# Two fused transformer layers on one core: dummy products before the first rows, a quantized up group moved behind the third down tile, and one copy moved to VectorE

## The chip, the cores and the metric

The kernel runs on one NeuronCore of a Trainium2 chip. The core has a matrix engine (TensorE, PE in the profile), three elementwise engines (VectorE = DVE, ScalarE = ACT, GpSimd = POOL) and SyncE (SP), which issues the DMA transfers. The metric is the device time of one execution in microseconds (us), taken as the median of several runs. Every engine runs its own instructions in the order of the program and waits for the others through semaphores.

## The reference, cut to what matters

Four blocks follow each other on x of 2 batches x 512 rows x 512 columns, all in float32. Each block ends with a residual addition and a layer norm.

```python
x = norm(x + attn0(x))   # linear attention: q = elu(x Wq + bq) + 1, then (q M) / (q z), then Wo
x = norm(x + ffn0(x))    # ternary weights: trunc(clip(128 * silu(gate) * up)), down, trunc(clip)
x = norm(x + attn1(x))   # one head of 128: softmax(q k^T / sqrt(128)) v, then Wo and a bias
x = norm(x + ffn1(x))    # silu(x Wg) * (x Wu), then Wd, in full float32 weights
```

## The kernel before, in words

A batch is four tiles of 128 rows. TensorE contracts over partitions, so every block first transposes its rows (products with an identity matrix into PSUM, then a copy to SBUF) and then runs the products with the weights. PSUM has eight buffers, shared by all products in turn (`psum`, line 68). The order of the work on PE, ACT, DVE and SP comes from a scheduler, which sorts the instructions by its own idea of when each could run; GpSimd's order is that of the source (`manual_schedule`, line 59). Once sorted, each engine keeps its order whatever happens.

**The start (lines 80 to 123 and 270 to 325).** SP issues the loads of the four row tiles of batch 0, of `bq` and `z` (128 x 8 each), and of the eight query weights `wq`. PE transposes the row tiles as they land (line 110, 16 transposes into four PSUM buffers), ACT and DVE copy two of the four buffers each (lines 121 and 123), and the query products follow (line 316). `bq` is first read by ACT (line 321), `z` by a copy on POOL (line 310).

**The end of the quantized feed-forward (lines 506 to 662).** `up(b, c)` is one group of 128 (the last: 96) of the 1376 inner columns for batch b: 16 products for gate and up, then on ACT a silu (529), on DVE a product (532) and a cut (149), on ACT two truncating conversions (159, 160) and on DVE their sum (539). `f0_down(i)` issues the down product of row tile i (0 to 3 are batch 0, 4 to 7 batch 1; 11 products, line 569) and keeps a pipeline going behind it:

- `scaled(i)`: ACT scales the sum out of PSUM (586) and DVE cuts it (149);
- `added(i - 1)`: ACT converts twice (159, 160), DVE combines them to `w` (594), POOL subtracts `w` from the rows (595);
- `layernorm_stats` of tile i - 2 on DVE (129, 131), with the root on POOL (137, 138);
- `layernorm_apply` of tile i - 3 on DVE (143).

The rows of batch 0 are then transposed for the next attention (`xt_a1`, line 110), copied (121, 123) and multiplied by the query and key weights (line 746).

**The second attention (lines 735 to 885).** For each batch the probabilities are transposed (`pt_p`), `values` multiplies them with v into one PSUM buffer (line 814) and copies the result to `ot` (line 818, on ACT for both batches), and four `output` products (line 831) follow. `attended` adds the residual and takes the norm's statistics on DVE (836, 129, 131); the root and offset are made on POOL (137, 138, 825, 826), and ACT applies the norm (827). `split_rows(0)` then transposes the normed rows of batch 0 (line 860) and cuts them into parts on DVE and ACT (669, 688 to 690) for the last feed-forward's products (line 906).

Of the kernel before, what the change touches and what calls it, by code (L numbers as in the profile page):

```python
# [19 lines left out]
P = 128  # L20
# [16 lines left out]
def kernel(  # L37
# [19 lines left out]
    nc = tc.nc  # L57
# [10 lines left out]
    def psum(name):  # L68
        return ps.tile([P, 512], F32, tag="mm", name=name)
# [4 lines left out]
    def load_x(b):  # L74
        for t in range(NT):
            x = xp.tile([P, HID], F32, tag="x", name=f"x_{b}_{t}")
            nc.sync.dma_start(x, x_in[b, ts(t, P), :])
            xs[b].append(x)

    load_x(0)  # L80
    bq = const.tile([D, NH], F32, tag="bq", name="bq")
    nc.sync.dma_start(bq, bq_in)
    z = const.tile([D, NH], F32, tag="z", name="z")
    nc.sync.dma_start(z, z_in)

    ident = const.tile([P, P], F32, tag="ident", name="ident")
    make_identity(nc, ident)
# [7 lines left out]
    nc.vector.memset(below_half, -BELOW_HALF)  # L95
    ones = const.tile([P, P], F32, tag="ones", name="ones")
    nc.vector.memset(ones, 1.0)


    copies = []  # L100
# [25 lines left out]
    def layernorm_stats(row, name):  # L126

        st = small.tile([P, 6], F32, tag="st", name=f"st_{name}")
        nc.vector.bn_stats(st, row)
        mv = small.tile([P, 2], F32, tag="mv", name=f"mv_{name}", bufs=8)  # L130
        nc.vector.bn_aggr(mv, st)
        return root(mv, name)
# [8 lines left out]
    def layernorm_apply(out, row, stats):  # L141
        mv, rstd = stats
        nc.vector.tensor_scalar(
            out, row, mv[:, 0:1], rstd, ALU.subtract, ALU.mult
        )
# [76 lines left out]
    def branch(flag):  # L222
        return nc.values_load(flag[0:1, 0:1], engines=[PE], min_val=0, max_val=1)
# [44 lines left out]
    def query_tile(name):  # L268
        return wqp.tile([P, 2, HID], F32, tag="wq", name=name)

    with tc.tile_pool(name="a0w", bufs=1) as a0w, tc.tile_pool(name="a0", bufs=2) as a0:
        wq = []
        for h in range(NH):
            if h % 2 == 0:
                two = query_tile(f"wq{h}").rearrange("p a (k d) -> p a k d", k=NK)
            w = two[:, h % 2]
            nc.sync.dma_start(w, wq_in[h])
            wq.append(w)
        load_x(1)
        m = a0w.tile([D, NH, D], F32, tag="m", name="m")  # L280
        nc.sync.dma_start(m, m_in)
# [169 lines left out]
        order = [(b, t) for b in range(B) for t in range(NT)]  # L451
# [49 lines left out]
    with tc.tile_pool(name="f0", bufs=2) as f0:  # L501
# [7 lines left out]
        def up(b, c):  # L509
            n = CHUNKS[c][1]  # L510
            t = ts_up[c]
            pp = [psum(f"pg_f0{b}_{c}"), psum(f"pu_f0{b}_{c}")]
            with tc.If(ternary_up > 0) as way:
                for a in range(2):
                    for i in range(2 * NK):
                        nc.tensor.matmul(  # L516
                            pp[a][:n], t[:, a, i % NK, :n], x2[b][i],
                            start=(i == 0), stop=(i == 2 * NK - 1),
                        )
            with way.Else():  # L520
                for a in range(2):
                    for i in range(2 * NK):
                        nc.tensor.matmul(
                            pp[a][:n], gus[c][:, a, i % NK, :],
                            x2[b][i].bitcast(F32),
                            start=(i == 0), stop=(i == 2 * NK - 1),
                        )
            sg = fp.tile([P, S], F32, tag="sg", name=f"sg_f0{b}_{c}")
            nc.scalar.activation(sg[:n], pp[0][:n], AF.Silu, scale=silu_scale[:n])
            y = f0.tile([P, S], F32, tag="y", name=f"y_f0{b}_{c}")  # L530

            step = nc.vector.scalar_tensor_tensor(
                y[:n], sg[:n], eff_up[:n, 1:2], pp[1][:n], ALU.mult, ALU.mult
            )
            cut_to_12(y[:n])
            ta, tb = truncated_parts(f0, y[:n], n, f"f0{b}_{c}")

            it = its[b][c // 4][:, c % 4]
            nc.vector.scalar_tensor_tensor(  # L539
                it[:n], tb[:n], 128.0, ta[:n], ALU.min, ALU.subtract  # L540
            )
            inter[b].append(it)
            if to_divide:
                part = to_divide.pop(0)
                if part:
                    divided(*part)
            return step
# [16 lines left out]
        def down(b, t):  # L564
            pd = psum(f"pd_f0{b}_{t}")
            last = len(CHUNKS) - 1
            with tc.If(ternary_d > 0) as way:
                for c, (_, n) in enumerate(CHUNKS):
                    nc.tensor.matmul(  # L569
                        pd, inter[b][c][:n, ts(t, P)], td[c][:n].bitcast(F32R),  # L570
                        start=(c == 0), stop=(c == last),
                    )
            with way.Else():
                for c, (_, n) in enumerate(CHUNKS):
                    nc.tensor.matmul(
                        pd, inter[b][c][:n, ts(t, P)].bitcast(F32), wds[c][:n],
                        start=(c == 0), stop=(c == last),
                    )
            return pd
# [4 lines left out]
        def scaled(i):  # L584
            y = f0.tile([P, HID], F32, tag="y", name=f"yd_{i}")
            nc.scalar.activation(y, pds[i], AF.Copy, scale=down_scale)
            cut_to_12(y)
            ys[i] = y

        def added(i):  # L590
            b, t = order[i]
            ta, tb = truncated_parts(f0, ys[i], P, f"d{i}")
            w = fp.tile([P, HID], F32, tag="sg", name=f"w_{i}")
            nc.vector.scalar_tensor_tensor(w, tb, 128.0, ta, ALU.min, ALU.subtract)  # L594
            nc.gpsimd.tensor_sub(xs[b][t], xs[b][t], w)  # L595

        def f0_down(i):
            if i < len(order):
                pds[i] = down(*order[i])
                scaled(i)  # L600
            if 0 <= i - 1 < len(order):
                added(i - 1)
            if 0 <= i - 2 < len(order):
                b, t = order[i - 2]
                stats[i - 2] = layernorm_stats(xs[b][t], f"f0_{i - 2}")
            if 0 <= i - 3 < len(order):
                b, t = order[i - 3]
                layernorm_apply(xs[b][t], xs[b][t], stats[i - 3])
# [30 lines left out]
        nc.vector.tensor_scalar(down_scale, eff_d, -128.0, None, ALU.mult)  # L639
        up(1, 9)  # L640
        ternary_d = branch(flag_d)
        f0_down(0)
        f0_down(1)
        up(1, 10)
        for i in range(2, len(order) - 1):
            f0_down(i)
        xt_a1 = [transposed(xs[0], "a10")]
        for i in range(len(order) - 1, len(order) + 3):
# [83 lines left out]
    for b in range(B):  # L732
# [10 lines left out]
        for j in range(2):  # L743
            p = psum(f"pqk_{b}_{j}")
            for k in range(NK):
                nc.tensor.matmul(  # L746
                    p, wqkv[:, k, ts(j, D)], xt[:, k, :],
                    start=(k == 0), stop=(k == NK - 1),
# [7 lines left out]
        for t in range(NT):  # L756
            p = psum(f"pv_{b}_{t}")
            for k in range(NK):
                nc.tensor.matmul(  # L759
                    p[:, :D], xt[:, k, ts(t, P)], wqkv[:, k, ts(2, D)],  # L760
                    start=(k == 0), stop=(k == NK - 1),
# [49 lines left out]
    def values(b, pt):  # L811
        po = psum(f"pot_{b}")
        for k in range(NT):
            nc.tensor.matmul(
                po, qkv[b][2][:, k, :], pt[:, k, :], start=(k == 0), stop=(k == NT - 1)
            )
        ot = ot2[:, b, :]
        nc.scalar.copy(ot, po)
        ots.append(ot)

    def scalar_norm(x, stats, name):
# [32 lines left out]
    def split_rows(b, room):  # L854
# [9 lines left out]
        return parts  # L864

    values(0, pt0)
    pt1 = transposed(probs[1][0], "p1")
    for t in range(NT):
        attended(0, t, output(0, t))
    values(1, pt1)  # L870
    sums1 = [output(1, t) for t in range(NT)]
    rooms = [rows_room(0, "r0"), None]
# [221 lines left out]
```

## Time and profile before

| | us |
|---|---|
| median of 3 runs | 492.82 (492.47 to 493.49) |
| the profiled execution, whole | 495.07 |
| its span, from first to last instruction | 493.3 |
| PE busy | 475.6 (96%) |
| DVE busy | 350.4 (71%) |
| ACT busy | 272.1 (55%) |
| POOL busy | 127.3 (26%) |
| granted clock of TensorE, mean | 0.991 |

The profiled execution is 2.25 us longer than the median of the runs. All start times are counted from the start of its span. A row of a timeline gives start, duration, engine, line, operation, what is written and read, and how often; in brackets stands how long the engine had been idle and what ended that. A float32 product with 512 columns appears as two matmul instructions of about 0.43 us each from start to start.

### The profile page before, as it was taken

The page shows a single profiled execution, that of the slowest core. Times are in us where ns is not written, and L with a number is a line of the kernel's source. Part 1 is how long each engine was busy: PE and PEld are TensorE (multiplying, and loading weights), DVE is VectorE, ACT ScalarE, POOL GpSimd, SP SyncE. Part 2 cuts the span into 40 slices and gives each one's busy share as a digit, 9 for nine tenths or more (in the row PEclk, how much of TensorE's full clock was granted, in tenths as well). Part 3 has the DMA queues.
Part 4 walks back from the last instruction along what each step waited for, and adds up shares of the span by engine and source line. Part 5 has one row for each costly group of instructions (what it writes and reads, how often), then busy time and mean ns, then how long its engine had stood idle before and what let it go on. Part 6 is the DMA issues. An engine that isn't in the chain of part 4 may idle for free.

```text
span 493.3 us, 5751 instructions
## 1 busy us (share of the span) xinstructions
PE 475.6 (96%) x1859; PEld 325.1 (66%) x1859; DVE 350.4 (71%) x672; ACT 272.1 (55%) x507; POOL 127.3 (26%) x163
## 2 busy tenths in 40 slices
PE   6999999999999999999899978999999999999995
PEld 4454444434577788777566536788778888888885
DVE  1374677677675576846869968888876697999852
ACT  1444899565677576456545933556655565433220
POOL 0253102666520194003874033000000000023211
PEclk9999999999999999999999989999999999999998
DMA  8999600000060001121670000000000000000111
GB/s 280 400 361 355 238 1 0 1 0 1 2 200 31 3 1 45 46 87 33 203 282 2 0 0 1 1 0 2 0 1 0 1 1 1 1 21 23 43 45 43
DMA packets 13749, 33.99 MB, mean 69 GB/s; under 512 B 1872, under 2 KB 2768, under 8 KB 13712
## 3 DMA queue, kind: packets, MB, share of 16 engines
q1 hardware_dynamic: 13568, 33.37, 18.9%
q8 instruction: 22, 0.36, 0.3%
q10 hardware_dynamic: 144, 0.13, 0.1%
q14 instruction: 15, 0.12, 0.1%
HBM read 31.40 MB, written 2.10 MB: 68 GB/s over the span
## 4 chain that ended last, share of the span: by engine, by line
PE 65%; DVE 9%; ACT 8%; issue 3%; POOL 2%; POOLq 0%; DVEq 0%; ACTq 0%
PE pm L906 16%; PE pdm L981 8%; PE pu_f L516 8%; PE pg_f L516 8%; PE pc L906 8%; PE pdc L981 4%; DVE x L382 4%; PE pqk L746 3%; ACT y L373 2%; ACT t L392 2%; PE pd_f L569 2%; PE pv L759 1%; PE psc L773 1%; PE po L360 1%; ACT den L364 1%
## 5 line engine op out<-in xcount | busy, mean ns | idle before, releaser
L360 PE MATMUL po<-mw,q 128*128 128x512 f32 x128 | 56.7, 597 | 1.1 <-DVE x L382 0.9
L316 PE MATMUL pq<-xt_a,wq 128*128 128x512 f32 x128 | 57.3, 600 | 0.0
L360 PEld LDWEIGHTS po<-mw,q 128*128 128x128 f32 x128 | 23.2, 189 | 33.2 <-issue 18.9
L316 PEld LDWEIGHTS pq<-xt_a,wq 128*128 128x128 f32 x128 | 24.4, 193 | 30.0 <-issue 27.8
L137 POOL TENSOR_TENSOR rstd_f<-mv_f,ln_eps 128x1 f32<-128x1 f32 x16 | 4.0, 252 | 139.9 <-DVE mv_f L992 137.6
L906 PE MATMUL pm<-r,it_early 128*128 128x512 f32 x144 | 38.2, 394 | 0.2
L906 PE MATMUL pm<-r,ugu 128*128 128x512 f32 (+1 forms) x144 | 36.8, 393 | 0.0
L382 DVE SCALAR_TENSOR_TENSOR x<-po,den,x 128x511 f32<-128x511 f32 x40 | 29.8, 746 | 2.0
L906 PEld LDWEIGHTS pm<-r,it_early 128*128 128x128 f32 x144 | 26.9, 188 | 6.6 <-ACT r L688 0.4
L906 PEld LDWEIGHTS pm<-r,ugu 128*128 128x128 f32 (+1 forms) x144 | 26.8, 186 | 6.3
L159 ACT ACTIVATE ta_f<-y_f,below_half 128x512 int8<-128x512 f32 (+1 forms) x22 | 15.9, 722 | 25.8 <-DVE y_f L149 25.5
L917 DVE SCALAR_TENSOR_TENSOR ev_q<-pm,ev_q 128x512 f32<-128x512 f32 (+1 forms) x28 | 19.2, 687 | 14.0 <-PE pm L906 14.0
L377 POOL TENSOR_TENSOR y<-y,y 128x511 f32<-128x511 f32 x16 | 20.3, 1271 | 32.1 <-ACT y L373 31.3
L394 POOL TENSOR_SCALAR td<-wd,inv_down 128x512 fp32r<-128x512 f32 (+1 forms) x11 | 19.5, 1791 | 30.3 <-DVE inv_down L193 30.3
L539 DVE SCALAR_TENSOR_TENSOR it_f<-tb_f,ta_f 128x512 fp32r<-128x512 int16 (+1 forms) x22 | 15.1, 688 | 15.8 <-ACT tb_f L160 15.8
L906 PE MATMUL pc<-r,ugu 128*128 128x512 f32 (+1 forms) x96 | 26.0, 393 | 0.0
L321 ACT ACTIVATE e<-pq,bq 128x512 f32<-128x512 f32 x16 | 11.1, 691 | 26.8 <-PE pq L316 26.8
L516 PE MATMUL pg_f<-xh,tu 128*128 128x512 f32 (+1 forms) x88 | 25.6, 407 | 0.0
L516 PE MATMUL pg_f<-xl,tu 128*128 128x512 f32 (+1 forms) x88 | 24.4, 395 | 0.1
L516 PE MATMUL pu_f<-xh,tu 128*128 128x512 f32 (+1 forms) x88 | 24.0, 394 | 0.0
L516 PE MATMUL pu_f<-xl,tu 128*128 128x512 f32 (+1 forms) x88 | 23.9, 393 | 0.0
L595 POOL TENSOR_TENSOR x<-x,w 128x512 f32<-128x512 f32 x8 | 12.6, 1573 | 40.5 <-DVE w L594 40.5
(280 smaller groups left out, 1118.7 us busy)
## 6 DMA issues: line engine op xcount, KB each, us to landing
gu<-in_gu SPq DMA_DIRECT2D x20, 512.0 KB, 7.7
wo<-in_wo SPq DMA_DIRECT2D x16, 512.0 KB, 7.1
wd<-in_wd SPq DMA_DIRECT2D x20, 256.0 KB, 5.3
x<-in_x SPq DMA_DIRECT2D x8, 256.0 KB, 4.8
wq<-in_wq SPq DMA_DIRECT2D x8, 256.0 KB, 4.7
out<-x SPq DMA_DIRECT2D x7, 256.0 KB, 2.0
gu<-in_gu SPq DMA_DIRECT2D x2, 384.0 KB, 6.5
wqkv<-in_wqkv SPq DMA_DIRECT2D x1, 768.0 KB, 10.8
```

The costliest lines, as they stand in the source:

```text
L159: nc.scalar.activation(a[:n], y, AF.Relu, bias=below_half[:n])
L316: nc.tensor.matmul(pq, wq[h][:, k, :], xt[:, k, :], start=(k == 0), stop=(k == NK - 1))
L360: nc.tensor.matmul(po, qs[b][h0 + j][:, ts(t, P)], mw[:, h0 + j, :], start=True, stop=True,)
L377: nc.gpsimd.tensor_add(ys[0][:, :LAST], ys[0][:, :LAST], y[:, :LAST])
L382: steps.append(nc.vector.scalar_tensor_tensor(x[:, :LAST], four[j][:, :LAST], d, x[:, :LAST], ALU.mult, ALU.add))
L394: eng.tensor_scalar(out, w, factor, None, ALU.mult)
L516: nc.tensor.matmul(pp[a][:n], t[:, a, i % NK, :n], x2[b][i], start=(i == 0), stop=(i == 2 * NK - 1),)
L539: nc.vector.scalar_tensor_tensor(it[:n], tb[:n], 128.0, ta[:n], ALU.min, ALU.subtract)
L746: nc.tensor.matmul(p, wqkv[:, k, ts(j, D)], xt[:, k, :], start=(k == 0), stop=(k == NK - 1),)
L906: nc.tensor.matmul(p[:n], w, x, start=(left[id(p)] == begun[id(p)]), stop=(left[id(p)] == 1))
L917: nc.vector.scalar_tensor_tensor(ev[:n], pm, MAIN, ev[:n], ALU.mult, ALU.add)
L981: nc.tensor.matmul(p[:, :w], got[j // 4][1][kind][:n, j % 4], down_parts[j][kind][:, cols], start=(j == 0 and kind == kinds[0]), stop=(j = ...
```

## The change

Three edits:

1. Nine float32 products of a 128 x 128 tile of ones with itself are put ahead of the first transposes, into a PSUM buffer `rise` that nobody reads. The loads of `bq` and `z` are issued behind the first query weight instead of ahead of it.
2. `up(1, 10)`, the last up group of batch 1, is called behind `f0_down(2)` instead of behind `f0_down(1)`.
3. The copy of the attended values of batch 1 out of PSUM is made by VectorE instead of ScalarE.

```diff
     load_x(0)
     bq = const.tile([D, NH], F32, tag="bq", name="bq")
-    nc.sync.dma_start(bq, bq_in)
     z = const.tile([D, NH], F32, tag="z", name="z")
-    nc.sync.dma_start(z, z_in)
...
     ones = const.tile([P, P], F32, tag="ones", name="ones")
     nc.vector.memset(ones, 1.0)
+    rise = psum("rise")
+    for _ in range(9):
+        nc.tensor.matmul(rise[:, :P], ones, ones, start=True, stop=True)
...
             nc.sync.dma_start(w, wq_in[h])
             wq.append(w)
+            if h == 0:
+                nc.sync.dma_start(bq, bq_in)
+                nc.sync.dma_start(z, z_in)
...
         ternary_d = branch(flag_d)
-        f0_down(0)
-        f0_down(1)
+        for i in range(3):
+            f0_down(i)
         up(1, 10)
-        for i in range(2, len(order) - 1):
+        for i in range(3, len(order) - 1):
             f0_down(i)
...
         ot = ot2[:, b, :]
-        nc.scalar.copy(ot, po)
+        (nc.vector.tensor_copy if b else nc.scalar.copy)(ot, po)
```

The scheduler's order changes beyond the moved lines. PE differs only by the nine products and the moved group. DVE and ACT get a new order in the whole stretch of the down tiles. With w4 for line 594 of row tile 4 and so on, DVE's order around the last tiles of batch 0 is:

```
before: bn2(129) cut4(149) mv2(131) apply1(143) cut5 bn3 w4(594) mv3 apply2 cut6 bn4 w5 mv4 apply3 w6 copies k1,k3(123) cut7 bn5
after:  bn2 w3 mv2 apply1 bn3 apply2 cut4 mv3 cut5 w4 cut6 bn4 w5 mv4 apply3 cut7 bn5 copies k1,k3 w6
```

On ACT the copies of the transposed rows (line 121, k = 0 and 2) stand ahead of the first conversion of tile 7 in the old order, and behind it in the new one. At the start, DVE adds the second pair of output weights (line 339) after one more query step than before. The copy of edit 3 stands on DVE directly behind the statistics of row tile 3 of batch 0.

## The prediction, made before the changed kernel was run

> **What bounds the kernel.** The page has PE at work 96% of the span, and 65% of the chain that ended last is PE. So I read PE's own waits first: only there, and where its clock is low, can a change that takes no work away win time.
>
> ```profile
> engine line waited for: us in total, times, longest us
> PE pt_a L110 <- DMA x<-in_x: 3.8, 2, 3.6
> PE po L831 <- ACT ot L818: 2.5, 1, 2.5
> PE pt_a L110 <- DVE x L143: 2.0, 1, 2.0
> PE pt_f L860 <- ACT x L827: 1.0, 1, 1.0
> ```
>
> The three edits sit on the three longest waits: the rows' first load, the transposes behind the down tiles, the copy `ot`. Second, the timeline of PE at the start:
>
> ```profile
> 3.59 1.94 PE L110 MATMUL pt_a<-ident,x 128*128 128x128 f32 x8 [3.59 <-DMA x<-in_x]
> 5.75 1.97 PE L110 MATMUL pt_a<-ident,x 128*128 128x128 f32 x8 [0.22 <-DMA x<-in_x]
> 7.75 18.27 PE L316 MATMUL pq<-xt_a,wq 128*128 128x512 f32 x40
> 25.86 1.04 PE L333 MATMUL pt_m<-ident,m 128*128 128x128 f32 x8
> ```
>
> Eight transposes take 1.94 us at 3.59 and 1.04 us at 25.86. Weight loads of the query products take 337 ns up to 8.77 and 190 ns from 9.55. So PE runs at half speed until about 9.5, though the granted clock is written as 1.00 there. Third, the table of stretches around the copy (the clock is the third number from the end):
>
> ```profile
> 292.00:292.50 0.50, 0.35 (x1) 0.30 (x2) 0.00 (x0) 0.41 (x2) 0.16 (x1) 1.00 0.00 0
> 292.50:293.00 0.50, 0.50 (x2) 0.24 (x1) 0.00 (x0) 0.50 (x1) 0.00 (x0) 0.77 0.00 0
> 293.00:293.50 0.50, 0.50 (x2) 0.06 (x1) 0.00 (x0) 0.01 (x1) 0.00 (x0) 0.50 0.00 0
> ...
> 296.00:296.50 0.50, 0.50 (x2) 0.28 (x1) 0.30 (x2) 0.00 (x0) 0.12 (x1) 0.81 0.00 0
> ```
>
> After the 2.5 us pause the clock is halved for some 3.5 us. The same table shows 0.50 from 245.0 to 248.4, behind the pause at 241.3. The pause of 1.0 us at 307 lowers nothing. A long pause is paid twice.
>
> **Edit 3, the copy.** The last `pot` product ends at 289.65, and PE goes on at 292.15. Why, the rows of ACT and DVE show:
>
> ```profile
> 290.81 0.81 ACT L827 ACTIVATE x<-x,off_a,rstd_a 128x512 f32<-128x512 f32 x1 [0.58 <-POOL off_a L826]
> 291.53 0.57 ACT L818 COPY ot<-pot 128x512 f32<-128x512 f32 x1
> ```
>
> ```profile
> 289.27 0.18 DVE L131 BATCH_NORM_AGGREGATE mv_a<-st_a 128x2 f32<-128x6 f32 x1
> 293.75 0.75 DVE L836 SCALAR_TENSOR_TENSOR x<-po,sums,x 128x512 f32<-128x512 f32 x1 [4.30 <-PE po L831]
> ```
>
> On ACT the copy stands behind a norm that waits for POOL. On DVE it lands in 4.3 us of idleness. DVE's copy of such a tile (line 123) takes 0.69: 289.70 + 0.69 + 0.06 = 290.45, so PE resumes 1.7 sooner. The pause left is 0.8, shorter than the harmless one at 307. The four `po` products then take 8 x 0.43 = 3.44 instead of the 5.23 from 292.15 to 297.38, 1.8 less. PE gets 3.5, but DVE goes on as bound: residuals at 291.45, 292.75 and 293.45, two statistics between, and the first cut (669) at 294.75 + 0.1 against 298.06, 3.2 sooner. The first norm of batch 1 (ACT, 827) keeps ACT's cast (688) to 295.8 against 298.77, and the first product of line 906 waits for it: **-3.0**. DVE works without a pause from there to 307.5, and every later wait hangs on it. Had the clock not dropped before, only the 1.65 of the wait would go: -1.6 is the other end.
>
> **Edit 2, the moved group.** It does the same PE work before tile 3 (220.7 to 229.6), so down tile 3 ends when it did. What counts is when the norm of row tile 3 is applied, which PE waits for from 241.3 to 243.27. DVE's rows before:
>
> ```profile
> 236.00 0.42 DVE L149 TENSOR_SCALAR yd<-yd 128x512 int32<-128x512 int32 x1
> 236.34 0.16 DVE L131 BATCH_NORM_AGGREGATE mv_f<-st_f 128x2 f32<-128x6 f32 x1
> 236.43 1.42 DVE L143 TENSOR_SCALAR x<-x,mv_f,rstd_f 128x512 f32<-128x512 f32 x1
> 237.77 0.41 DVE L149 TENSOR_SCALAR yd<-yd 128x512 int32<-128x512 int32 x1
> 238.10 0.68 DVE L129 BATCH_NORM_STATS2 st_f<-x 128x6 f32<-128x512 f32 x1
> 238.71 0.67 DVE L594 SCALAR_TENSOR_TENSOR w<-tb_d,ta_d 128x512 f32<-128x512 int16 x1
> ```
>
> The cut of tile 4 (236.00) is long done when `w4` starts at 238.71; then come POOL's subtraction of tile 4 (to 241.37), behind it POOL's root for tile 3 (to 242.16), and apply3 at 242.70. That root stands behind tile 4's subtraction in the source, so PE's wait really hangs on `w4`.
>
> In the new order cut4 stands behind apply2. Step by step: group 10's products end on PE at 227.1; DVE's product, bn1, cut: 228.9; ACT's four conversions and two scalings at 0.61 spacing: tile 2 converted at 232.0; `w2` 232.7; subtraction 1.3: 234.1; bn2 and `w3` (now behind bn2) 235.4; subtraction of tile 3, 1.9 to 2.2 where a DVE apply starts just before it (rows at 239.45, 233.15): 237.4 to 237.7, as before (237.57). But from there: root 0.8, apply2 0.5, cut4 0.4, two conversions 1.3, handovers 0.1, so `w4` at 240.5 to 240.8 instead of 238.71. The rest of the chain as before or 0.5 shorter (a subtraction of 1.3 instead of 1.9): the transposes of tile 3 start at 244.75 to 245.3, **1.5 to 2.0 later**. Then ACT's copy k = 0 stands behind a conversion that waits for cut7, itself behind apply3: 0.4 more if DVE gets in ahead of POOL, 1.7 if it waits as lines 149 and 143 did at 230.72 and 236.43 (1.16 and 1.42 instead of about 0.45). The query products of line 746 start 1.9 to 3.7 later; I take 2.2, near the lower end, for the back-to-back rows at 239.39 and 239.82 show DVE slipping in. PE's pause grows from 2 us to some 5, so the halved clock reaches further into these products: from 0.7 less to 1.0 more than the 1.9 lost now, I take 0.3. Sum **+2.5**, bounds +1.2 to +4.7. Below that, a gain is possible only if POOL's stretched subtractions (1.9, 2.2) all shrink to 1.3: then up to -0.5.
>
> **Edit 1, the start.** PE can begin when `ones` is written, 1.10. Nine products are 18 instructions; the v products (line 759, 32 in 3.73) take 0.112 each, at half speed 0.224: 4.0 us, to 5.2. The transposes begin there, not at 3.59. What pays for that is the clock: PE is at work 2.4 us sooner. The halved stretches of this trace last 3.4 us (245.0 to 248.4; 292.7 to 296.2), and counted back in such steps from 245.0 there is a step at 6.07, one before 9.5. With full speed from 6.07: 3.6 transposes by then, the thirteenth (the last that copy k = 0 needs) at 6.07 + 9.4 x 0.107 = 7.1, copy 0.6, queries from 7.9 at full speed, against 7.75 with 0.87 lost up to 9.5: **-0.7**. Best: full speed at 5 or sooner, rows bounding (tile 3 lands before 6.7): queries from 7.3, -1.3. Worst: still 9.5, transposes to 9.1: +0.5.
>
> The rule that speaks against this edit stands in the Trainium skill, "TensorE: Matmul & The Clock Gate", Part 1: the clock is judged in free-running windows of 3413 ns, so that the moment of release varies from run to run; by Part 4 transposes do not count as PE work. The stretches of 3.4 us agree with the window; no row here tests the second. By it nine products (4.0) hold a full window only by luck, and the edit would be worth +0.5 in most runs.
>
> From 7.75 to 125.9 PE waits for nothing, and ACT (from 51.1) starts on a PE result, so the gain is carried. Costs hidden: `bq` and `z` arrive about 0.5 later, first read at 12.33 and, on POOL, 6.80, where the next work is at 19.07; SP's other issues behind them keep their places, the first `wq` is 0.95 sooner. The buffer of `rise` is free at 5.2 and shifts the turn of the eight by one; PE shows no wait for a buffer but 0.9 at 125.9 (line 382), so I price it at 0, bounds -0.3 to 0.3. DVE's reordering at 20 moves nothing PE waits for (first fold at 42.2).
>
> **Sum.** -0.7 + 2.5 - 3.0 = **-1.2** against the profiled execution: 495.07 (span 493.3 and 1.77 around it) to 493.9. The median of the runs is 2.25 lower; taken off it the forecast is **491.6**.
>
> **Rivals.**
> 1. *The moved group costs nothing*: POOL's subtractions run at 1.3 throughout, and tile 3 is normed when it was. Then -0.7 - 3.0 = -3.7: 489.1. For it: four of eight subtractions took 1.3 to 1.5. Against: cut4 stands behind apply2 whatever POOL does.
> 2. *Slower: the pause at 241 decides*. cut7 waits for POOL (+3.7 at the query products) and the clock stays halved one stretch longer (+1.0): +4.7, with the start at -0.7 and the copy at -1.6 because the clock mostly did not drop there: +2.4, 495.2. It decides once the products of line 746 start over 3.0 later than now while the copy gives under 2.5.
> 3. *The clock parts are luck of one execution*: the runs without a profile are 2.25 shorter; without the drops the copy gives -1.6, the start about 0, the moved group +2.2: +0.6, 493.4.
> That the code does not do what it says is excluded: the new order of each engine has all three.
>
> **Chances.** Under 0.2% (1.0 us) this measurement cannot tell from no change. The forecast case (-2.4 to 0) 0.45, of it 0.25 faster and 0.20 same; rival 1 0.22, faster; rival 2 0.23, 0.21 slower and 0.02 same; rival 3 0.10, 0.06 same and 0.04 slower. Sums: faster 0.47, same 0.28, slower 0.25. The range 488.9 to 494.9 leaves out the ends of rivals 1 and 2.
>
> **What would show it.** Start: query products before 7.75 and weight loads of 190 ns from the first; wrong if transposes begin after 5 and the loads stay at 337 ns. Copy: the gap ahead of line 831 under 1 us and the clock at 1.00 behind it. Moved group: the wait of the transposes for line 143 growing from 2.0 to 3.5 or more; if it shrinks, the step on cut4 is wrong. The forecast fails most easily there.

## The result, and the profile after

The changed kernel takes 493.49 us (493.13 to 493.81, 6 runs) against 493.25 (492.47 to 493.68, 6 runs) for the kernel before: ratio 1.0006, 95% interval 0.9993 to 1.0019. That is no difference that can be measured. The forecast was 491.6 in a range of 488.9 to 494.9: the time lies in the range, 1.9 us above the forecast, and almost on the 493.4 of rival 3, which had a chance of 0.10.

In the two profiled executions the picture is another. The span went from 493.3 to 492.0, 1.3 us shorter, close to the -1.2 of the sum. TensorE's waits after (the line numbers shown are 3 to 6 higher than before):

```profile
engine line waited for: us in total, times, longest us
PE pt_a L113 <- DVE x L146: 3.1, 1, 3.1
PE rise L100 <- DVE ones L95: 1.2, 1, 1.2
PE pt_f L866 <- ACT x L833: 1.0, 1, 1.0
...
PE po L837 <- DVE ot L824: 0.8, 1, 0.8
```

The wait for the rows' first load is gone from the list, the wait for row tile 3 has grown from 2.0 to 3.1, and the wait for the copy `ot` has shrunk from 2.5 to 0.8. TensorE's timeline at the start:

```profile
1.15 4.07 PE L100 MATMUL rise<-ones 128*128 128x128 f32 x18 [1.15 <-DVE ones L95]
5.06 2.35 PE L113 MATMUL pt_a<-ident,x 128*128 128x128 f32 x16
7.76 17.43 PE L322 MATMUL pq<-xt_a,wq 128*128 128x512 f32 x40 [0.35 <-ACT xt_a L124]
25.03 1.04 PE L339 MATMUL pt_m<-ident,m 128*128 128x128 f32 x8
```

The query products begin when they did (7.76 against 7.75), but the same forty are through 0.84 us sooner: `pt_m` begins at 25.03 instead of 25.86. The down products carry that on (214.75 for 215.55). Behind row tile 3:

```profile
243.57 0.86 PE L113 MATMUL pt_a<-ident,x 128*128 128x128 f32 x4 [3.09 <-DVE x L146]
245.13 9.88 PE L752 MATMUL pqk<-xt_a,wqkv 128*128 128x512 f32 x16 [0.70 <-ACT xt_a L124]
```

The sixteen query and key products of batch 0 take 9.88 us; before they took 8.95:

```profile
244.27 8.95 PE L746 MATMUL pqk<-xt_a,wqkv 128*128 128x512 f32 x16 [0.35 <-ACT xt_a L121]
```

The table of stretches (clock third from the end) says why:

```profile
244.00:245.00 1.00, 0.44 (x3) 0.50 0.81 305
...
249.00:250.00 1.00, 1.00 (x2) 0.50 1.03 410
250.00:251.00 1.00, 1.00 (x3) 0.65 1.02 406
```

The clock is halved from about 243.9 to 250.7, 6.8 us, twice as long as the 3.4 us of before. At the copy, in contrast, it stays at 1.00, and the eight instructions of the output products take 3.70 instead of 5.40 (first line: before):

```profile
292.15 5.40 PE L831 MATMUL po<-wo,ot 128*128 128x512 f32 x8 [2.50 <-ACT ot L818]
292.23 3.70 PE L837 MATMUL po<-wo,ot 128*128 128x512 f32 x8 [0.78 <-DVE ot L824]
```

So from trace to trace: start -0.8, moved group +2.6 (the v products behind line 752 at 254.85 for 253.06, from -0.8 to +1.8), copy -3.0 (VectorE's first cut into `m_x` at 296.83 for 298.06, so from +1.8 to -1.2). Sum -1.2. Before and after:

```profile
298.06 1.27 DVE L669 TENSOR_SCALAR m_x<-pt_f 128x512 int32<-128x512 int32 x2
296.83 1.27 DVE L675 TENSOR_SCALAR m_x<-pt_f 128x512 int32<-128x512 int32 x2
```

The question is why the runs show nothing of it.

### The profile page after: what moved, and what is told of

It is laid out like the page before. It is cut to its first block, busy times and chain, and to the rows that moved or that the text cites. A ratio compares the mean times of both kernels' runs of the same rounds, so it can differ in the third digit from the quotient of the medians.

```text
span 492.0 us, 5789 instructions
## 1 busy us (share of the span) xinstructions
PE 476.4 (97%) x1877; PEld 327.3 (67%) x1877; DVE 350.6 (71%) x673; ACT 271.3 (55%) x506; POOL 126.6 (26%) x163
## 4 chain that ended last, share of the span: by engine, by line
PE 68%; DVE 8%; ACT 8%; issue 3%; POOL 1%; POOLq 0%; DVEq 0%; ACTq 0%
PE pm L912 16%; PE pdm L987 8%; PE pu_f L522 8%; PE pg_f L522 8%; PE pc L912 8%; PE pdc L987 4%; PE pd_f L575 4%; DVE x L388 4%; PE pqk L752 3%; ACT y L379 2%; ACT t L398 2%; PE pv L765 1%; PE pot L820 1%; PE psc L779 1%; PE po L366 1%
## 5 line engine op out<-in xcount | busy, mean ns | idle before, releaser
L601 POOL TENSOR_TENSOR x<-x,w 128x512 f32<-128x512 f32 x8 | 11.5, 1438 | 44.7 <-DVE w L600 44.7
```

## The experiments

All times are set against runs of the kernel before on the same chip. Its medians on the three chips used were 493.9 to 494.1 (26, 29 and 23 runs, from 491.9 to 497.7), so 0.1% is 0.49 us. The changed kernel was not run again beside them. Where an experiment is compared with the changed kernel, or with an experiment on another chip, the difference given is that of the two ratios.

### Each edit alone, and the two that gained

`e1_start`, `e2_group` and `e3_copy` are the kernel before with one of the three edits of the diff above; `e4_start_copy` has the first and the third.

> Edit 1 alone (dummy products and the two moved loads). Theory A (the three terms of the forecast hold, but a halved clock behind a pause comes and goes from run to run, and the one profiled execution of before had more of it than most): -0.7 us against before, between -1.3 and +0.5; first memory transposes (pt_m) at 25.0 instead of 25.9. Rival B (the terms are not real: the group moves for nothing and what the copy wins is waited away later): also -0.7, this run does not tell them apart. Rival C (the dummy products delay the rows by as much as the clock gains): 0 +- 0.3.

> Edit 2 alone (last up group behind the third down tile). Theory A: +1.5 to +2.8 us against before: the transposes of row tile 3 wait 3.1 us for line 143 instead of 2.0, the copy k = 0 stands behind the conversion of tile 7, and the clock is halved behind the pause. Rival B: 0 +- 0.5, the later start is made up before the end.

> Edit 3 alone (copy of the attended values of batch 1 on VectorE). Theory A: -1.6 us where the clock did not drop behind the old pause, -3.0 where it did, so -1.6 to -2.5 in the median; the pause ahead of line 831 is 0.8 us and the clock stays at 1.00 behind it. Rival B: under 0.5 either way, the gain is waited away between 297 and 310.

> Edits 1 and 3 without edit 2. Theory A: the sum of the two, -2.0 to -3.5 us against before, and so about 2 to 3 us faster than the changed kernel. Rival B: 0 to -0.7, as fast as the changed kernel.

| | us (median) | ratio to before, 95% | in us |
|---|---|---|---|
| e1_start | 492.61 | 0.9971 (0.9950 to 0.9993) | -1.4 (-2.5 to -0.3) |
| e2_group | 497.81 | 1.0075 (1.0044 to 1.0106) | +3.7 (+2.2 to +5.2) |
| e3_copy | 491.49 | 0.9949 (0.9929 to 0.9968) | -2.5 (-3.5 to -1.6) |
| e4_start_copy | 490.55 | 0.9930 (0.9902 to 0.9958) | -3.5 (-4.8 to -2.1) |

The single edits add up to -0.2, the whole change measured +0.3 (-0.3 to +0.9). That agrees, although each of the three intervals reaches 1.0 to 1.5 us to either side. The change is therefore two gains and one loss of the same size: the moved group alone eats what the other two bring. That it is free (rival 1) is excluded. The two gaining edits together are the fastest kernel of this study, 490.55.

### The dummy products alone, the loads alone

`e6_dummies` has the nine products of ones without the later loads, `e11_loads` the later loads without the products.

> The kernel before with the nine products of ones at the start alone; the loads of bq and z stay where they were. Theory A (the gain of the first edit is the full clock in the query products, and the later loads matter little): 0.5 to 1.4 us shorter than the kernel before, the products of pt_m begin by 25.1. Rival (the gain comes from the first weights being asked for 2 DMAs earlier): within 0.3 us of the kernel before.

> The kernel before with the loads of bq and z behind the first query weights, and no products of ones. Theory A (of the first edit only the products count): within 0.4 us of the kernel before. Rival (the rest of the first edit's gain, 1.4 against 0.9 with the products alone, is the loads'): 0.4 to 0.8 us shorter.

e6_dummies: 492.76, ratio 0.9981 (0.9968 to 0.9994), -0.9 us. e11_loads: 494.35, ratio 1.0004 (0.9987 to 1.0021), +0.2 us. What the first edit gains comes from the products; the later loads gain nothing that can be seen (-0.6 to +1.0 us).

### The kernel before, profiled again

> The kernel before once more, unchanged, for a second profiled execution. Theory A (the losses of clock differ between executions of the same kernel): the two waits are as in the first profile, 1.98 and 2.50 us, to 0.1; the sixteen query products and the eight output products are not both as long as there (8.95 and 5.40 us). Rival (both losses are in every execution): 8.95 and 5.40 again, to 0.3.

This execution took 492.25, span 490.5, against 495.07 and 493.3 in the first profile, with the same program. Its waits and its timeline at the three places:

```profile
PE po L831 <- ACT ot L818: 2.5, 1, 2.5
PE pt_a L110 <- DVE x L143: 2.0, 1, 2.0
```

```profile
24.76 1.04 PE L333 MATMUL pt_m<-ident,m 128*128 128x128 f32 x8
...
242.33 1.09 PE L110 MATMUL pt_a<-ident,x 128*128 128x128 f32 x4 [1.99 <-DVE x L143]
243.46 8.28 PE L746 MATMUL pqk<-xt_a,wqkv 128*128 128x512 f32 x16
...
290.66 3.70 PE L831 MATMUL po<-wo,ot 128*128 128x512 f32 x8 [2.49 <-ACT ot L818]
```

The two long waits are the same to 0.01 us. What differs is the clock: `pt_m` begins 1.1 us sooner with no dummy products at all, the stretch with the query products is 0.5 shorter, and behind the very same 2.49 us of waiting the output products take 3.70, not 5.40. That makes 3.3. Of this 0.2 is lost again by the down products (they begin 0.94 sooner, at 214.61 for 215.55) and 0.4 behind the copy, since the products of line 906 now wait 0.9 us for a cast that in the slower execution was ready. So the 2.8 us between two executions of one kernel come from these three places, and each of the three edits works on one of them. Theory A holds.

### The pause filled instead of removed

`e5_fill` is the changed kernel with 13 more products of ones, which nothing reads, behind the transposes of row tile 2 (`third` is the last of them):

```diff
+            if name == "a10" and k == NK - 1:
+                with tc.issue_after(third.ins):
+                    fill = psum("fill")
+                    for _ in range(13):
+                        nc.tensor.matmul(fill[:, :P], ones, ones, start=True, stop=True)
```

> The changed kernel with 13 more products of ones (nothing reads them) put on TensorE between the transposes of row tile 2 and those of row tile 3 of the second batch, about 12 x 0.22 = 2.6 us of work inside the 3.09 us in which TensorE waits for row tile 3. The wait itself isn't shortened. Theory A (the pause costs twice: once as waiting, once because the granted clock is halved for some 6.9 us behind it): the halving goes, the sixteen query products take about 7.3 us instead of 9.88, the run is 2.0 to 2.9 us shorter than the changed kernel, about 490.6 to 491.5. Rival (only the waiting costs, the clock would have fallen in most runs of either kernel anyway or is hidden): within 0.5 us of the changed kernel.

Measured 491.0, ratio 0.9948 (0.9934 to 0.9962): -2.6 against before, so 2.9 less than the changed kernel by the ratios, the top end of what was expected (2.5 less by the medians). TensorE's timeline there:

```profile
241.25 2.84 PE L127 MATMUL fill<-ones 128*128 128x128 f32 x24
243.93 0.60 PE L113 MATMUL pt_a<-ident,x 128*128 128x128 f32 x4
...
251.85 3.73 PE L770 MATMUL pv<-wqkv,xt_a 128*128 128x128 f32 x32
```

The transposes of row tile 3 begin 0.36 later than in the changed kernel (243.93 for 243.57; half of that is the later start), but from there to the v products it is 7.92 us, against 11.28 in the changed kernel. The products of ones take no time off the wait; they keep the clock, which is granted at 1.00 throughout this stretch.

`e9_before_fill` does the same to the kernel before, with 8 products at row tile 3 and 10 ahead of the output products; `e10_fill4` puts 8 into the kernel with edits 1 and 3.

> The kernel before, none of the three edits, with products of ones that nothing reads inside its two longest pauses of TensorE: 8 ahead of the transposes of row tile 3 (pause 1.98 us) and 10 between the attended values and the output products (pause 2.50 us). Neither wait is shortened. Theory A (the clock falls behind these two pauses in some executions and not in others; the profiled execution of before lost 1.8 us of clock in the sixteen query products and 1.7 in the eight output products, a typical execution perhaps half of it): query products 7.1 to 7.6, output products 3.7, the median 0.7 to 2.2 us below the kernel before, the runs within 1.5 us of one another. Rival (typical executions lose nothing, the profiled one was an exception): within 0.4 us of the kernel before.

> The first and the third edit, not the second, with 8 products of ones that nothing reads in the 1.98 us pause ahead of the transposes of row tile 3. Theory A: the clock stays full behind that pause in all executions, 489.4 to 490.4, that is 0 to 1 us below the same kernel without the fill, and some 1.1 us (the 3.09 against the 1.98 us of waiting) below the changed kernel with its pause filled. Rival (the moved group costs by its clock alone, not by the longer wait): the same as the changed kernel with its pause filled, about 491.

Both forecasts missed. e9_before_fill: 493.63, ratio 0.9993 (0.9976 to 1.001), -0.3 us, with runs from 492.5 to 494.8. e10_fill4: 491.0, ratio 0.9945 (0.9926 to 0.9965), which is 0.7 above the same kernel without the fill by the ratios, and level with e5_fill. The clock did stay: the query products take 7.13 in both. But the fill moved the order. TensorE of e10_fill4:

```profile
238.96 0.66 PE L112 MATMUL pt_a<-ident,x 128*128 128x128 f32 x4 [1.40 <-DVE x L150]
239.45 0.39 PE L126 MATMUL fill<-ones 128*128 128x128 f32 x2
239.60 2.81 PE L579 MATMUL pd_f<-td,it_f 128*128 128x512 f32 x11
242.25 1.72 PE L126 MATMUL fill<-ones 128*128 128x128 f32 x14
```

The scheduler now put the transposes of row tile 2, and one fill product, ahead of down tile 7 (line 579) instead of behind it. TensorE waits 1.40 us for row tile 2 there, and the down products, the fill and the transposes of row tile 3 follow 1.5 us later than without the fill (243.81 for 242.84, though the start was 0.57 sooner). Row tile 3 itself was ready at 242.23 (VectorE applies its norm from 241.71 on, for 0.52); what comes late is TensorE's own queue. That eats what the clock gave. In e9_before_fill it is 1.4, against the second profile of before; what the fills save there is, in the mean of the table below, 1.3 and 0.8, so some 0.7 should be left, and the interval of -1.2 to +0.5 leaves room for that. Both times came out at the rival's number, but the reason of the rival in e9_before_fill, that typical executions lose no clock, does not hold: its twelve runs have a mean granted clock of 0.996 to 0.999, while 48 of the 78 runs of the kernel before have 0.991 or less. In e5_fill, where the moved group delays row tile 3 anyway, the same displacement cost 0.2. Whether the longer wait of the moved group by itself is worth its 1.1 us these runs can't say.

### The queue on VectorE

`e8_cutfirst` is the changed kernel with each application of the norm placed behind the cut of the down tile after it:

```diff
-                layernorm_apply(xs[b][t], xs[b][t], stats[i - 3])
+                with tc.issue_after(cuts[min(i, 7)].ins):
+                    layernorm_apply(xs[b][t], xs[b][t], stats[i - 3])
```

> The changed kernel with each row tile's last step of the layer norm placed on VectorE behind the rounding of the down tile after it, so that the rounding of down tile 4 is not queued behind the application to row tile 2. Theory A (the later w4, and with it the 1.1 us longer wait for row tile 3, comes from that queue): the wait for row tile 3 falls from 3.09 us to about 2.0, and the run is 1.0 to 2.5 us shorter than the changed kernel (1.1 of waiting, and up to 1.4 of the halved clock). Rival (the down products themselves, which begin later because the group was moved behind them, set the end of row tile 3): wait 3.0 or more, within 0.5 us of the changed kernel.

Measured 491.94, ratio 0.9966 (0.9953 to 0.9979): -1.7 against before, 2.0 less than the changed kernel by the ratios. The wait fell to 2.33, not to the 2.0 expected. VectorE of the changed kernel, then of e8_cutfirst:

```profile
237.66 0.42 DVE L152 TENSOR_SCALAR yd<-yd 128x512 int32<-128x512 int32 x1
237.99 0.17 DVE L134 BATCH_NORM_AGGREGATE mv_f<-st_f 128x2 f32<-128x6 f32 x1
238.08 0.39 DVE L152 TENSOR_SCALAR yd<-yd 128x512 int32<-128x512 int32 x1
239.48 0.69 DVE L600 SCALAR_TENSOR_TENSOR w<-tb_d,ta_d 128x512 f32<-128x512 int16 x1 [1.00 <-ACT tb_d L163]
```

```profile
237.34 0.39 DVE L152 TENSOR_SCALAR yd<-yd 128x512 int32<-128x512 int32 x1
...
239.14 0.69 DVE L601 SCALAR_TENSOR_TENSOR w<-tb_d,ta_d 128x512 f32<-128x512 int16 x1
```

The cut of tile 4 (first line) came 0.32 sooner, with a start 0.43 later; `w4` (last line) 0.34 sooner, so 0.77 in all, and the wait shrank by 0.76. The wait for row tile 3 follows `w4` one for one, so the queue on VectorE is shown to be the cause of most of its growth. In this execution the clock also stays at 1.00 behind the wait (8.90 us to the v products instead of 11.28); seven of its twelve runs, with a mean clock of 0.992 to 0.993, still lose some. The rest of the growth stays, because the cut still stands behind the statistics of row tile 3, which wait for POOL.

`s1_swap` tries to remove the wait in the kernel with edits 1 and 3, by placing the statistics of tile i - 2 (and so POOL's root) ahead of the addition of tile i - 1:

```diff
-            if 0 <= i - 1 < len(order):
-                added(i - 1)
             if 0 <= i - 2 < len(order):
                 b, t = order[i - 2]
                 stats[i - 2] = layernorm_stats(xs[b][t], f"f0_{i - 2}")
+            if 0 <= i - 1 < len(order):
+                added(i - 1)
```

> The first and the third edit without the second, and one more: in the down stage the statistics of row tile i-2 are placed ahead of the addition to row tile i-1, so that the root for row tile 3 is not queued on GpSimd behind the subtraction of the next tile. Theory A (TensorE waits 2.0 us for row tile 3 and loses about 1 us of clock behind it in the kernel with these two edits): the wait falls below 1 us and the run is 1.2 to 3.0 us shorter than the kernel with the first and third edit alone (490.55), 487.5 to 489.3. Rival (something else is late next: the last row tiles' additions, then pushed back on VectorE): the wait moves to another row tile and the time stays within 0.5 us of 490.55.

It missed by the sign: 494.17, ratio 1.0005 (0.9994 to 1.0017), 3.7 us above the kernel it should have improved. Its VectorE and its TensorE:

```profile
234.78 0.69 DVE L131 BATCH_NORM_STATS2 st_f<-x 128x6 f32<-128x512 f32 x1 [1.71 <-POOL x L600]
...
238.63 0.69 DVE L131 BATCH_NORM_STATS2 st_f<-x 128x6 f32<-128x512 f32 x1 [1.97 <-POOL x L600]
```

```profile
242.68 1.20 PE L112 MATMUL pt_a<-ident,x 128*128 128x128 f32 x6 [1.75 <-DVE x L145]
...
257.85 1.64 PE L112 MATMUL pt_a<-ident,x 128*128 128x128 f32 x13 [1.75 <-DVE x L145]
```

Statistics directly behind POOL's subtraction leave VectorE idle for the whole subtraction, tile after tile (1.71, 1.97), with `w4` queued behind it. The wait at row tile 3 hardly shrinks (1.75), and a new one of 1.75 appears at row tile 3 of batch 1 (the fourth transpose behind 255.61). The rival named the move to another row tile, but neither it nor theory A had the time.

## Why the prediction was right or wrong

The same places in all fourteen profiles, in us. "Clock up" is where the trace's first record of the granted clock begins, at 1.00. "To v" is from the transposes of row tile 3 to the v products, which holds the query products: 7.9 with the pause filled, 8.4 in e6_dummies and e4_start_copy, where the pause is not filled and the clock stays at 1.00. "Halved" is how long the granted clock is 0.50 around these products. The last column is the output products.

| | clock up | `pt_m` begins | wait, row tile 3 | to v | halved | wait, `ot` | output |
|---|---|---|---|---|---|---|---|
| before | 9.46 | 25.86 | 1.98 | 9.79 | 3.4 | 2.50 | 5.40 |
| e12_before | 6.88 | 24.76 | 1.99 | 9.25 | 3.4 | 2.49 | 3.70 |
| e11_loads | 9.38 | 25.93 | 2.00 | 9.73 | 3.4 | 2.49 | 5.40 |
| e6_dummies | 5.82 | 25.01 | 1.99 | 8.39 | 0 | 2.50 | 3.70 |
| e1_start | 4.96 | 26.03 | 1.99 | 9.37 | 3.4 | 2.50 | 5.26 |
| e3_copy | 6.85 | 25.01 | 1.99 | 9.21 | 3.4 | 0.78 | 3.70 |
| e4_start_copy | 6.63 | 25.41 | 1.99 | 8.38 | 0 | 0.78 | 3.70 |
| e2_group | 7.26 | 24.95 | 3.09 | 10.78 | 6.8 | 2.50 | 5.40 |
| after | 4.95 | 25.03 | 3.09 | 11.28 | 6.8 | 0.78 | 3.70 |
| e5_fill | 5.64 | 25.21 | filled | 7.92 | 0 | 0.78 | 3.70 |
| e10_fill4 | 5.47 | 24.84 | filled | 7.92 | 0 | 0.79 | 3.70 |
| e9_before_fill | 11.53 | 26.99 | filled | 7.91 | 0 | filled | 3.70 |
| e8_cutfirst | 6.85 | 25.52 | 2.33 | 8.90 | 0 | 0.78 | 3.70 |
| s1_swap | 4.16 | 24.98 | 1.75 | 9.36 | 3.4 | 0.79 | 3.70 |

**The start: the gain as forecast, by a clock that came up elsewhere.** The nine products took 4.07 (forecast 4.0), the transposes began at 5.06 (5.2), the queries at 7.76 (7.9) at full speed (the first two weight loads take 0.30 together, each later one 0.19). The gain of 0.83 was forecast as 0.7. But the clock came up at 4.95, not at the 6.07 of the working. All sixteen transposes then ran at full speed, as in the best case of the prediction, and yet the queries did not begin sooner, because the transposes waited for row tiles 2 and 3:

```profile
6.09 0.42 PEld L113 LDWEIGHTS pt_a<-ident,x 128*128 128x128 f32 x4 [0.23 <-DMA x<-in_x]
6.75 0.42 PEld L113 LDWEIGHTS pt_a<-ident,x 128*128 128x128 f32 x4 [0.24 <-DMA x<-in_x]
```

The 6.07 fits the old execution, whose clock came up at 9.46, one step of 3.41 behind 6.05 (the working must have counted in steps of 3.413; in steps of 3.4, as it says, it would have come to 7.0). But each execution has its own steps: with the products the clock is up at 4.2 to 6.9, without them at 6.9 to 11.5. That is what the products do. From the first query product to `pt_m` it takes 17.3 us in all eight profiles with them, and 17.2 to 19.0 in the six without (three of them 17.2 or 17.3). How much of this shows at `pt_m` depends on when the rows land (the queries begin at 7.57 to 8.76 with the products). So the gain is a difference of two draws. Without the products the six profiles have `pt_m` at 24.76 to 26.99, mean 25.58; with them eight have 24.84 to 26.03, mean 25.25. That is -0.3, which does not stand out from such a spread; the runs say -0.9 (-1.6 to -0.3) for the products alone. The sign holds by the runs, the size lies somewhere between.

The rule weighed here, from the Trainium skill, "TensorE: Matmul & The Clock Gate", Part 4, that transposes do not count as PE work in the same way, is not what these runs show for the float32 transposes here, which the trace lists as MATMUL: in the second profile of before the clock is up at 6.88 and in e3_copy at 6.85, when TensorE had run nothing but transposes of rows (from 3.63 and 3.69 on). In e3_copy the last four of them start 0.11 us apart, the earlier ones 0.21. Part 1 there, that the moment of release differs from run to run, agrees: 24.76 and 25.86 are one and the same program.

**The moved group: the sum right by two errors.** Forecast +2.5, measured +2.6 between the traces and +3.7 (+2.2 to +5.2) alone. The step on `cut4` held: `w4` began at 239.48; with the 0.80 that the start had gained this is 240.28 against 238.71, 1.6 later (forecast 1.8 to 2.1). But the transposes of row tile 3 came only 1.1 later (wait 3.09 for 1.98), not 1.5 to 2.0, because POOL's subtraction behind `w4` took the shorter of the two lengths considered (second line, against the first, of before):

```profile
239.45 1.92 POOL L595 TENSOR_TENSOR x<-x,w 128x512 f32<-128x512 f32 x1 [0.86 <-DVE w L594]
240.25 1.27 POOL L601 TENSOR_TENSOR x<-x,w 128x512 f32<-128x512 f32 x1 [3.09 <-DVE w L600]
```

So the mark of 3.5 that was set for the wait was not reached. What was priced too low is the clock: 0.3 was taken for it, and the query products alone took 0.9 longer between the two traces. Behind 2.0 us of waiting the clock was halved for 3.4 us, in five of seven profiles; behind 3.09 us it was halved for 6.8 us, in both. That is the longer halving of rival 2, without its late cut. It is not luck of two profiles: the mean granted clock is 0.991 to 0.993 in all six runs of the changed kernel and 0.987 to 0.990 in all seven of e2_group, against 0.996 to 0.999 in the six of e5_fill. Seven kernels with the wait of 2.0 have 9.16 us from the transposes to the v products, the two with 3.09 have 11.03. So the group costs 1.1 of waiting and 1.9 behind it (of that up to 0.35 of waiting for the copy k = 0, the rest clock): +3.0, which the interval of e2_group holds.

**The copy: right.** The sign that it named for the copy came: PE's wait is 0.78 (forecast 0.8), the four output products ran at full clock, and `m_x` came 3.0 sooner, as forecast; alone the edit gave -2.5 (-3.5 to -1.6). The unsure part was named: -1.6 if the clock had not dropped. It drops behind the 2.5 us wait in four of the six profiles that have it (5.40, 5.40, 5.26, 5.40) and not in two (3.70). Behind 0.78 it drops in none of those with the copy on VectorE. A drop costs 1.7 in the output products and gives 0.5 back ahead of line 906, so in the mean the edit is worth, by this estimate, 1.7 of waiting and 4/6 x 1.2 = 0.8 of clock, -2.5, as measured.

**What failed: the last line of the sum.** "The median of the runs is 2.25 lower; taken off it the forecast is **491.6**." Up to that line the sum held: it gave 493.9 for the profiled execution, and the profiled execution of the changed kernel took 493.81. The terms were read off an execution of 495.07, which had lost clock in all three places; the change was credited with removing those losses, and then the sum was taken off a median of executions that had not all had them. The same loss was counted twice. The second profile of before, 2.8 us shorter by just these losses, shows that they come and go. The median of three runs was low besides: later runs on three chips have medians of 493.9 to 494.1.

Priced by the means above, the terms are -0.3 + 3.0 - 2.5 = +0.2, and the measurement says +0.3 (-0.3 to +0.9). This is an account made afterwards, and its -0.3 for the start is less than the -0.9 of the runs, so the close agreement is partly luck. Rival 3 had this total, +0.6, by other terms: it took the clock losses for luck of one execution, and they are a chance that differs from place to place. Of the 78 runs of the kernel before, 48 have a mean granted clock of 0.991 or less, as the first profile, 6 have 0.993 or 0.994, as the second, and 24 have 0.996 or more. Their time does not follow this clock closely, though (medians 494.17 for the 48 and 493.99 for the 24), and the granted clock does not show what the start loses: the profile of e9_before_fill has a mean of 0.996 and took 494.72, with the clock up only at 11.53.

**The costs at nothing held.** The loads did nothing that can be seen (e11_loads); the wait of 0.9 at 125.9 is the same after (0.86 us, at 125.10), so the buffer of `rise` cost nothing there.

**Why the clock falls behind a wait in one execution and not in another.** The records of the granted clock answer most of it. In all fourteen traces it changes only at whole steps of 3.413 us from where it first came up: in before at 9.46, then at 244.98 (69 steps later), 248.40 (70), 292.77 (83) and 296.18 (84). Cut along these steps, TensorE's busy time in before, after and e6_dummies is (length, busy, granted clock):

```profile
241.57:244.98 3.41, 1.36 (x6) 1.00 0.97 319
244.98:248.40 3.42, 3.42 (x5) 0.50 1.05 355
```

```profile
240.47:243.88 3.41, 0.32 (x4) 1.00 0.92 270
243.88:247.29 3.41, 2.71 (x7) 0.50 0.95 362
247.29:250.71 3.42, 3.42 (x5) 0.50 1.04 365
```

```profile
237.93:241.34 3.41, 2.55 (x16) 1.00 0.58 196
241.34:244.75 3.41, 1.79 (x7) 1.00 1.01 339
244.75:248.16 3.41, 3.41 (x8) 1.00 1.06 362
```

In before the wait of 1.98 us lies within one step, which is idle for 2.05 us, and the next step runs at half clock. In e6_dummies the same wait is cut in two by the step at 241.34, with 0.86 us of idle time on one side and 1.62 on the other, and the clock stays. In after the step behind the wait idles again (0.70 us, for the copy k = 0), and a second one is halved. So the wait decides together with where the steps lie, and each execution has its own steps. Open is what sets them, and how much idle time exactly lets the clock fall.

## What to carry to other kernels

Before a pause of TensorE is priced with the clock loss behind it, profile the same kernel a second time and look at where the clock's steps cut the pause: a loss that comes and goes is worth its chance times its size, and the sum belongs to the mean of the runs, not to the profile it was read from. A group moved to fill TensorE changes the queue of every engine that follows it; here it put one cut behind a norm, and TensorE's next wait grew by 1.1 us and cost 3. Where a wait can't be shortened, products that nobody reads can hold the clock through it, but look at the order they get: the same fill gained 2.9 us in one kernel and nothing in another, where it displaced real work by 1.5.

## What the runs showed of the hardware

- The granted clock changed only at whole steps of 3.413 us from its first rise, in all fourteen traces. Up to the last product it fell to 0.50 twelve times, in eight traces, each time behind a step in which TensorE had idled 1.94 to 3.09 us. Behind up to 1.63 us it never fell, and once (e12_before, 286.77 to 290.18) it did not fall behind 2.02. These idle times use the modelled ends of products, so a limit near 2.0 us is good to some 0.1. The rule in the Trainium skill, "TensorE: Matmul & The Clock Gate", Part 1, "HAM oscillation", is no idle gaps over about 3.4 us; here that is too lax.
- By wait: behind 2.0 us the clock fell in five of seven profiles, behind 2.5 us in four of six (1.6 to 1.7 us lost in the output products), behind the 0.8 us that the moved copy leaves in none of seven.
- After 3.09 and 0.70 us of waiting, with four transposes between, the halved stretch was 6.8 us, two steps; in e2_group it was 6.8 us too, with 1.16 us idle in the first of the two.
- Two executions of the same program, alike to 0.01 us in the two long waits, differ by 2.8 us, and 78 runs of the kernel before lie between 491.9 and 497.7.
- The granted clock is shown as 1.00 in the first 9 us of before although the products run at half speed there: the first record of it begins at 9.46, and ahead of that only durations show it.
